# A graph layer on one core: the weight matrix multiplied to each block's sum instead of to the gathered table

## The chip, the cores and the metric

The kernel runs on 1 core of a Trainium2 chip. The metric is the device time of one execution in microseconds (us). A core has five engines that run side by side, each through its own instruction queue in order: TensorE (PE; its weight loads are listed apart as PEld), VectorE (DVE), ScalarE (ACT), GpSimd (POOL) and SyncE (SP), the last of which here only issues transfers. Engines wait for each other through semaphores.

## What is computed

Two steps on a table x of 8192 rows and 512 columns. The first is a graph layer: every row is normalised, multiplied by a 512x512 matrix, and the rows of the result are summed along 131072 weighted edges. The second is a patch: some rows (by a mask on their normalised values) send two small vectors through a 7-layer network of width 160, and a one-hot vector of its result is added to 32 columns.

```python
def _L0_gnn_ref(x, weight, row, col, vals):
    h = jnp.einsum('nf,ef->ne', x, weight)
    msgs = vals[:, None] * h[col]
    return jax.ops.segment_sum(msgs, row, num_segments=8192)

x = x + _L0_gnn_ref(_layernorm(x), L0_gnn_weight, src, dst, edge_weight)
x = x + _L0_ffn_ref(_layernorm(x)[None], L0_ffn_W, L0_ffn_b)[0]
```

All of it is in 32-bit floats. The edges come sorted by `dst` (the row that is read), and `src` (the row that is added to) is in random order, so the kernel has to sort the edges by `src` itself.

## The kernel before

**Tiling.** 128 rows make a block; there are 64 (`NB`). A block's sum over its edges is taken in 17 tiles (`FT`) of 128 edges, so 1088 tiles in all (`NT`). Eight blocks make a unit (`U`), and the network runs once for each unit.

**Stage 1, groups (L208 to L264).** The edges lie as 128 partitions x 1024. `group(q)` sorts an eighth of them into cells by block: `hot` (L211, DVE) marks for each edge its block, `p_base` (L219, PE) counts the edges of the same block on earlier partitions, `cum` (L222 to L226, ACT then DVE) ranks the edges of a partition, `p_rank` (L229, PE) picks each edge's own rank out, `slot` and `at` (L232, L234, DVE) make a one-hot of the rank. Then in four chunks of two columns each: `blocks` (L244, ACT) copies a part of `hot` to 32-bit, turned so that the 64 block marks of one edge lie next to each other; `put` (L248, DVE, twice) multiplies the one-hot by the edges' addresses (`val_a`) and by their weights (`val_w`), also turned; and 64 small matmuls (L255, PE) drop the values into their cells in `p_c`. L262 copies the cells out.

**The projection (L269 to L296).** `project(b0)` handles two blocks: loads x, statistics on DVE (L275, L276), normalises on ACT (L283), transposes on PE (L287), copies on ACT (L289), multiplies by the matrix `gw` on PE (L292), copies on ACT (L295) and stores to the table `h_rows` in HBM (L296). `some(n)` emits n such pairs: one or two behind each group, two behind each of the bits below, and the rest at the end. Up to the gather stage the order of the instructions on each engine is a scheduler's.

**Stage 2, prefix (L310 to L400).** Each row of cells is compacted: free cells are counted by a scan, each filled cell gets the distance that it has to move, and eleven rounds (L353 to L368), one for each bit of that distance, move the words and weights by powers of two: `go` (L357), `stay` (L360) and two predicated copies on DVE, and a copy on ACT (L364). Then the fields are taken apart, turned by PE transposes (L391) and copied by ACT (L393, L398) to `at_dst`, `at_row` and `at_w`: for each tile, 128 addresses, 128 target rows and 128 weights. A flag `fits` says whether every row had room; a branch on it, ahead of the gather stage, chooses between `evenly()` and a general but slow path, `anyhow()`.

**Stage 3, gathers (L611 to L664).** `evenly()` goes over the 1088 tiles in an order that is written out by hand for PE, DVE and ACT. For tile t + AHEAD it issues the gather (`fetch`, L614: an indirect DMA on POOL's queue that brings 128 rows of `h_rows`) and makes `hot` (L618, DVE: a one-hot of the target rows times the weights); for tile t it multiplies (L655, PE; a 32-bit matmul runs as two instructions). After a block's last tile DVE adds the sum to x (L658) and takes the statistics (L608). Gathered tiles and hots live in a pool of 20 buffers. Behind every fourth tile one step of the network of the unit before is emitted: `ffn` is a generator, and each `yield` ends a step.

**The network (L417 to L575).** `ffn` normalises the unit's rows, finds the masked ones and gives them slots (L503: a matmul that counts them; L525: DVE takes the slot from it; L529: a one-hot `pick`; L536: matmuls that collect the rows), `layers` runs six layers over 128 columns x 4 quarters (32 of the 160 features go through `p_b` and `hb`, 128 through `p_a` and `ha`; each layer is two steps), and the result is scattered back (`p_o`, eight matmuls), added and stored, 2 MB for each unit.

Of the kernel before, what the change touches and what calls it, by code (L numbers as in the profile page):

```python
# [9 lines left out]
F32 = mybir.dt.float32  # L10
# [24 lines left out]
def tile_gnn_ffn(  # L35
# [49 lines left out]
    h_rows = dram.tile([N, D], F32, name="h_rows")  # L85
# [24 lines left out]
    fits = const.tile([1, 1], I32, name="fits")  # L110
# [8 lines left out]
    missed = const.tile([1, 1], I32, name="missed")  # L119
# [7 lines left out]
    w_in = const.tile([P, 1, GE], F32, name="w_in")  # L127
    wo_a = const.tile([P, 1, GB], F32, name="wo_a")
# [14 lines left out]
    nc.scalar.dma_start(b_out, ffn_bT[RESULT : RESULT + 1, L - 1 : L].to_broadcast([P, 1]))  # L143
    nc.scalar.copy(wo_a[:, 0, 0:1], w_a[:, L - 1, RESULT : RESULT + 1])
# [15 lines left out]
    ps_h = cell_ctx.enter_context(tc.tile_pool(name="ps_h", bufs=1, space=PSUM))  # L160
    gw = es.tile([P, KD, D], F32, name="gw")
    nc.scalar.dma_start(gw, gnn_wT.rearrange("(k p) e -> p k e", p=P))
# [45 lines left out]
    def group(q):  # L208
# [5 lines left out]

# [7 lines left out]
        nc.scalar.copy(cum[:, :, 0, :], p_base.rearrange("p i (b g) -> p (i b) g", g=GQ))  # L222
        for c in range(1, GC):
            nc.vector.tensor_tensor(cum[:, :, c, :], cum[:, :, c - 1, :], hot[:, :, c - 1, :],
                                    OP.add)
        nc.vector.tensor_tensor(cum, cum, hot, OP.mult)  # L226
        p_rank = ps_c.tile([P, CG], F32, name="p_rank")
        for b in range(NB):
            nc.tensor.matmul(p_rank, eye, cum[:, b].rearrange("p c g -> p (c g)"),  # L229
                             start=(b == 0), stop=(b == NB - 1))  # L230
        slot = ck.tile([P, 1, CG], BF16, name="slot", bufs=2)
# [8 lines left out]
        for c0 in range(0, GC, SUB):  # L240
            cg = slice(c0 * GQ, (c0 + SUB) * GQ)
            n = SUB * GQ
            blocks = ck.tile([P, n, NB], F32, name="blocks", bufs=2)
            nc.scalar.copy(blocks, hot[:, :, c0 : c0 + SUB, :].rearrange("p b c g -> p (c g) b"))  # L244
            put = ck.tile([P, n, 2, CAP], F32, name="put", bufs=2)
            for i, val in enumerate((val_a, val_w)):
                v = val[:, q, c0 : c0 + SUB, :].rearrange("p c (g o) -> p (c g) o", o=1)
                nc.vector.tensor_tensor(put[:, :, i, :], at[:, :, cg].rearrange("p s n -> p n s"),  # L248
                                        v.to_broadcast([P, n, CAP]), OP.mult)
            for k in range(n):  # L250
# [3 lines left out]
                for h in range(2):  # L254
                    nc.tensor.matmul(  # L255
                        p_c[h * NB : (h + 1) * NB, i, gl * CAP : (gl + 1) * CAP],
                        blocks[:, k, :],
                        put[:, k, :, :].rearrange("p i (s h) -> p h i s", h=2)[:, h],
                        start=False, stop=last)
        got = p_c[:, :, :width].rearrange("p i (g w s) -> p i g w s", w=2, s=HALF)  # L260
# [8 lines left out]
    def project(b0):  # L269
        xh = hp.tile([P, HG, D], F32, name="xh")  # L270
        nc.sync.dma_start(xh, rows_of(x, b0, HG))
        mv = hp.tile([P, HG, 2], F32, name="mv_h")
        for j in range(HG):
            st = hp.tile([P, 6], F32, name="mv_h_st")
            nc.vector.bn_stats(st, xh[:, j, :])  # L275
            nc.vector.bn_aggr(mv[:, j, :], st)  # L276
        rstd = rstd_of(hp, mv[:, :, 1], HG, "rstd_h")
        nmr = hp.tile([P, HG], F32, name="nmr_h")
        nc.vector.scalar_tensor_tensor(nmr, mv[:, :, 0], -1.0, rstd, op0=OP.mult, op1=OP.mult)
        for j in range(HG):  # L280
            b = b0 + j
            xn = hp.tile([P, D], F32, name="xn")
            nc.scalar.activation(xn, xh[:, j, :], AF.Identity, bias=nmr[:, j : j + 1],  # L283
                                 scale=rstd[:, j : j + 1])
            p_t = ps_h.tile([P, KD, P], F32, name="p_t")
            for k in range(KD):
                nc.tensor.transpose(p_t[:, k, :], xn[:, k * P : (k + 1) * P], ident)  # L287
            xnT = hp.tile([P, KD, P], F32, name="xnT")
            nc.scalar.copy(xnT, p_t)  # L289
            p_h = ps_h.tile([P, D], F32, name="p_h", bufs=2)  # L290
            for k in range(KD):
                nc.tensor.matmul(p_h, xnT[:, k, :], gw[:, k, :], start=(k == 0),  # L292
                                 stop=(k == KD - 1))
            hs = hp.tile([P, D], F32, name="hs")
            nc.scalar.copy(hs, p_h)  # L295
            nc.sync.dma_start(h_rows[b * P : (b + 1) * P, :], hs)  # L296


    pairs = iter(range(0, NB, HG))

    def some(n):
        for b0 in itertools.islice(pairs, n):
            project(b0)

    for q in range(NQ):
        group(q)
        some(1 + q % 2)
# [3 lines left out]
    with tc.tile_pool(name="sq", bufs=1) as sq, tc.tile_pool(  # L311
        name="ps_q", bufs=2, space=PSUM
    ) as ps_q:
# [24 lines left out]
        nc.vector.tensor_copy(fits, good[:, 3:4])  # L338
# [13 lines left out]
        bit = LOWS + DSTS  # L352
        while bit < 32:  # L353
            s = 1 << (bit - LOWS - DSTS)

            go = sq.tile([P, ROW], I32, name="go")
            nc.vector.tensor_scalar(go, word, 31 - bit, 31, op0=OP.logical_shift_left,  # L357
                                    op1=OP.arith_shift_right)
            stay = sq.tile([P, ROW], I32, name="word", bufs=2)
            nc.vector.scalar_tensor_tensor(stay, go, -1, word, op0=OP.bitwise_xor,  # L360
                                           op1=OP.bitwise_and)
            nc.vector.copy_predicated(stay[:, : ROW - s], go[:, s:], word[:, s:])
            w2 = post.tile([P, ROW], F32, name="w2", bufs=2)
            nc.scalar.copy(w2, wt)  # L364
            nc.vector.copy_predicated(w2[:, : ROW - s], go[:, s:], wt[:, s:])
            word, wt = stay, w2
            bit += 1
            some(2)  # L368
# [33 lines left out]
    late = ctx.enter_context(tc.tile_pool(name="late", bufs=1))  # L402

# [13 lines left out]
    def layers(fp, ps_a, ps_s, v, T):  # L417

        ha = hb = None
        for i in range(L - 1):  # L420
            p_b = ps_s.tile([P, T], F32, name="p_b")
            p_a = ps_a.tile([P, NG, 512], F32, name="p_a")[:, :, :T]
# [10 lines left out]
            if i == 0:  # L433
# [5 lines left out]
                for g in range(NG):  # L439
                    r = slice(GB * g, GB * g + 3)  # L440
                    nc.tensor.matmul(p_a[:, g, :], w_in[r, 0, 0:P], v[r, :], start=True, stop=True)
# [6 lines left out]
            for g in range(NG):  # L448
                nc.tensor.matmul(p_a[:, g, :], w_b[quads[g], i, 0:P], last_hb[quads[g], :],  # L449
                                 start=True, stop=False)  # L450
            yield
            for g in range(NG):
                nc.tensor.matmul(p_b[quads[g], :], w_a[:, i, P:GE], last_ha[:, g, :],  # L453
                                 start=False, stop=True)
            evict_b()
            for g in range(NG):
                nc.tensor.matmul(p_a[:, g, :], w_a[:, i, 0:P], last_ha[:, g, :], start=False,  # L457
                                 stop=True)
# [22 lines left out]
    def ffn(fp, ps_a, ps_s, u, xu, mv):  # L481
# [70 lines left out]
        for j in range(U):  # L552
# [6 lines left out]
        addv = add.rearrange("p (h s) i -> p h (s i)", s=NPOS)  # L559
        yield  # L560
        p_o = ps_a.tile([P, U // 2, 512], F32, name="p_a")[:, :, : 32 * NPOS].rearrange(
            "p q (h c) -> p q h c", h=2)
        for j in range(U):
            q, h = divmod(j, 2)
# [56 lines left out]
    def evenly():  # L621
        AHEAD, EVERY = 4, 4
        NU = NB // U
        with tc.tile_pool(name="xp", bufs=3) as xp, tc.tile_pool(name="gp", bufs=20) as gp, \
# [20 lines left out]
            for u in range(NU):  # L645
# [14 lines left out]
                for _ in work:  # L660
                    pass
# [183 lines left out]
```

## Time and profile before

| what | us |
|---|---|
| median of 3 runs (2211.91 to 2217.22) | 2213.83 |
| the profiled execution | 2220.42 |
| its span, first to last instruction | 2218.6 |
| last group's cells copied | 373.8 |
| eleven bits | 395.1 to 518.6 |
| last store to `h_rows` issued | 598.1 |
| first gather issued | 601.4 |
| last gather issued | 2158.6 |

| engine | busy us | instructions |
|---|---|---|
| PE | 1667.6 | 9559 |
| DVE | 938.6 | 2007 |
| ACT | 376.0 | 435 |
| POOL | 1048.8 | 1110 |

In a row of groups (line, engine, operation, tile it writes, tiles it reads, shape, count) the first number behind the bar is the busy time in us and the second the mean duration of one instruction in ns; PE's instructions overlap, so busy time divided by the count is what one costs there. Behind the second bar stands the engine's idle time ahead of these instructions, and what ended most of it. "Issue" is time in which the engine waited for nothing that the profile shows; "remote" is a release by something that the trace can't name. "Granted clock" is the share of its full clock that TensorE was granted; over the whole run it was 0.89. A row of a timeline has the start in us, the duration, the instruction, and in brackets the idle time before it and its releaser.

### The profile page before, as it was taken

To read this page: it belongs to the slowest core of one execution; us is meant where nothing else is said; L and a number is where in the kernel's file an instruction comes from. 1 tells how busy PE (TensorE), PEld (TensorE's weight loads), DVE (VectorE), ACT (ScalarE), POOL (GpSimd) and SP (SyncE) were. 2 spreads that over 40 slices of the span, in tenths; PEclk is the share of its full clock that TensorE was granted. 3 is DMA by queue.
4 is the path that set the end of the run, shared out by engine and by line. 5 is a ranking of instruction groups with operands and counts; after the bars stand their busy time and mean duration, and the time that the engine had idled before them with its cause. 6 is when DMAs were issued, how large, how long until landed. Compare 5 with 4: busy or idle time off the path is not lost.

```text
span 2218.6 us, 25506 instructions
## 1 busy us (share of the span) xinstructions
PE 1667.6 (75%) x9559; PEld 823.8 (37%) x9559; DVE 938.6 (42%) x2007; ACT 376.0 (17%) x435; POOL 1048.8 (47%) x1110
## 2 busy tenths in 40 slices
PE   4888888778675858785877788587778848787784
PEld 2666665334322323332433333242333314333332
DVE  7988987995112332323233233222322322232232
ACT  3564554454200000100000010001001000100101
POOL 2000000000166666666666666666666666666660
PEclk9999999899987978897988889798889879988986
DMA  3111101222386666676686667668666766766671
GB/s 116 40 35 40 44 26 40 87 95 98 117 280 186 189 181 181 209 230 185 182 262 176 185 197 245 183 177 263 180 184 192 249 180 180 224 190 178 181 223 41
DMA packets 125196, 357.94 MB, mean 161 GB/s; under 512 B 19964, under 2 KB 21768, under 8 KB 125064
## 3 DMA queue, kind: packets, MB, share of 16 engines
q0 software_dynamic: 87040, 285.28, 43.9%
q1 hardware_dynamic: 35120, 68.69, 8.9%
q10 hardware_dynamic: 2904, 2.21, 0.3%
q8 instruction: 83, 1.36, 0.3%
q14 instruction: 49, 0.40, 0.1%
HBM read 322.55 MB, written 33.55 MB: 161 GB/s over the span
## 4 chain that ended last, share of the span: by engine, by line
PE 30%; another core or an unknown queue 24%; DVE 9%; issue 5%; DMA 2%; POOL 1%; ACT 1%; DVEq 0%; POOLq 0%; ACTq 0%
PE p_g L655 26%; DVE hot L618 4%; PE p_a L457 2%; DMA xu<-in_x_dram 1%; POOL g L614 1%; DVE xu L658 1%; DVE st L608 1%; PE p_a L449 1%; DMA g<-h_rows,at_dst 1%; PE p_b L453 1%; PE p_b L446 1%; DVE ln L492 0%; DMA out_dram<-xu 0%; PE p_v L536 0%
## 5 line engine op out<-in xcount | busy, mean ns | idle before, releaser
L614 POOL DMA_INDIRECT g<-h_rows,at_dst x1088 | 1032.7, 949 | 731.1 <-issue 240.6
L655 PE MATMUL p_g<-g,hot 128*128 128x512 f32 x2176 | 1069.9, 645 | 235.2 <-issue 98.1
L655 PEld LDWEIGHTS p_g<-g,hot 128*128 128x128 f32 x2176 | 432.9, 207 | 794.5 <-issue 603.3
L618 DVE TENSOR_SCALAR hot<-lanes,at_row,at_w 128x128 f32<-128x128 f32 x1088 | 295.0, 360 | 43.7 <-issue 43.0
L292 PE MATMUL p_h<-gw,xnT 128*128 128x512 f32 x512 | 248.4, 626 | 47.1 <-ACT xnT L289 46.9
L658 DVE TENSOR_TENSOR xu<-xu,p_g 128x512 f32<-128x512 f32 x64 | 43.9, 686 | 542.5 <-remote 317.9
L321 POOL MEMSET zero<- 128x2560 bf16 x1 | 2.2, 2231 | 360.0 <-PE p_c L255 360.0
L255 PE MATMUL p_c<-put,blocks 128*64 128x40 f32 x4096 | 131.0, 234 | 38.8 <-DVE put L248 38.8
L292 PEld LDWEIGHTS p_h<-gw,xnT 128*128 128x128 f32 x512 | 94.9, 197 | 156.5 <-issue 92.3
L428 DVE TENSOR_SCALAR hb<-p_b,b_b 128x128 f32<-128x128 f32 x48 | 16.8, 351 | 314.7 <-remote 129.1
L255 PEld LDWEIGHTS p_c<-put,blocks 128*64 128x64 f32 x4096 | 127.6, 143 | 46.0 <-issue 23.8
L149 ACT ACTIVATE rstd_f<-mv_f,eps 128x8 f32<-128x8 f32 x8 | 2.4, 300 | 815.8 <-DVE st L608 392.1
L244 ACT CAST blocks<-hot 128x2048 f32<-128x2048 bf16 x32 | 126.2, 3945 | 69.7 <-PE p_c L255 64.3
L431 ACT ACTIVATE ha<-p_a,b_a 128x512 f32<-128x512 f32 x48 | 33.0, 687 | 419.1 <-PE p_g L655 191.5
L248 DVE TENSOR_TENSOR put<-at,val_a 128x1280 f32<-128x1280 bf16 x32 | 81.0, 2531 | 0.1
L248 DVE TENSOR_TENSOR put<-at,val_w 128x1280 f32<-128x1280 bf16 x32 | 75.7, 2364 | 0.0
L295 ACT COPY hs<-p_h 128x512 f32<-128x512 f32 x64 | 37.5, 586 | 144.3 <-PE p_h L292 79.4
L275 DVE BATCH_NORM_STATS2 mv_h_st<-xh 128x6 f32<-128x512 f32 x64 | 41.9, 682 | 46.5 <-DMA xh<-in_x_dram 46.4
L446 PE MATMUL p_b<-hb,w_b 32*32 32x128 f32 x320 | 18.9, 311 | 49.8 <-DVE hb L428 49.7
L283 ACT ACTIVATE xn<-xh,nmr_h,rstd_h 128x512 f32<-128x512 f32 x64 | 52.4, 824 | 4.1 <-issue 2.3
L457 PE MATMUL p_a<-ha,w_a 128*128 128x128 f32 x320 | 49.4, 296 | 3.4 <-issue 3.4
L546 ACT COPY back<-p_v 128x256 f32<-128x256 f32 x8 | 3.0, 372 | 287.0 <-PE p_v L544 212.1
(154 smaller groups left out, 950.9 us busy)
## 6 DMA issues: line engine op xcount, KB each, us to landing
g<-h_rows,at_dst POOLq DMA_INDIRECT x1088
xh<-in_x_dram SPq DMA_DIRECT2D x32, 512.0 KB
h_rows<-hs SPq DMA_DIRECT2D x64, 256.0 KB
xu<-in_x_dram SPq DMA_DIRECT2D x16, 1024.0 KB
out_dram<-xu SPq DMA_DIRECT2D x8, 2048.0 KB
gw<-in_gnn_wT_dram ACTq DMA_DIRECT2D x1, 1024.0 KB
w_a<-in_ffn_wT_dram ACTq DMA_DIRECT2D x1, 560.0 KB
w_b<-in_ffn_wT_dram ACTq DMA_DIRECT2D x4, 140.0 KB
```

Of the source, the lines that this page charges most:

```text
L244: nc.scalar.copy(blocks, hot[:, :, c0 : c0 + SUB, :].rearrange("p b c g -> p (c g) b"))
L248: nc.vector.tensor_tensor(put[:, :, i, :], at[:, :, cg].rearrange("p s n -> p n s"), v.to_broadcast([P, n, CAP]), OP.mult)
L255: nc.tensor.matmul(p_c[h * NB : (h + 1) * NB, i, gl * CAP : (gl + 1) * CAP], blocks[:, k, :], put[:, k, :, :].rearrange("p i (s h) -> p h ...
L275: nc.vector.bn_stats(st, xh[:, j, :])
L283: nc.scalar.activation(xn, xh[:, j, :], AF.Identity, bias=nmr[:, j : j + 1], scale=rstd[:, j : j + 1])
L292: nc.tensor.matmul(p_h, xnT[:, k, :], gw[:, k, :], start=(k == 0), stop=(k == KD - 1))
L446: nc.tensor.matmul(p_b[quads[g], :], w_b[quads[g], i, P:GE], last_hb[quads[g], :], start=True, stop=False)
L457: nc.tensor.matmul(p_a[:, g, :], w_a[:, i, 0:P], last_ha[:, g, :], start=False, stop=True)
L614: nc.gpsimd.indirect_dma_start(out=g, out_offset=None, in_=h_rows, in_offset=bass.IndirectOffsetOnAxis(ap=dst_ap, axis=0))
L618: nc.vector.tensor_scalar(hot, lanes, row_ap, w_ap, op0=OP.is_equal, op1=OP.mult)
L655: nc.tensor.matmul(p_g, hot, g, start=(k == 0), stop=(k == FT - 1))
L658: nc.vector.tensor_add(xu[:, j, :], xu[:, j, :], p_g)
```

## The change

**The matrix.** The table in HBM, now `n_rows`, holds the normalised rows of x without the matrix. The block's sum in the gather stage is copied out of PSUM by ACT (`z`), turned by four PE transposes, copied by ACT again (`zT`), and multiplied by `gw` into `p_y`; DVE adds `p_y` to x and takes the statistics. These are four steps of a generator, `block`, of which one is emitted behind every fourth tile, together with one step of the network. Hots and gathers are six tiles ahead instead of four, in 16 buffers instead of 20. `gw` is loaded after the prefix.

```diff
+    def weigh(fp, ps_w, xj, z, mv, j):
+        p_t = ps_w.tile([P, KD, P], F32, name="p_t")
+        for k in range(KD):
+            nc.tensor.transpose(p_t[:, k, :], z[:, k * P : (k + 1) * P], ident)
+        zT = fp.tile([P, KD, P], F32, name="zT")
+        nc.scalar.copy(zT, p_t)
+        yield
+        p_y = ps_w.tile([P, D], F32, name="p_y")
+        for k in range(KD):
+            nc.tensor.matmul(p_y, zT[:, k, :], gw[:, k, :], start=(k == 0), stop=(k == KD - 1))
+        yield
+        nc.vector.tensor_add(xj, xj, p_y)
+        st6 = fp.tile([P, 6], F32, name="st6")
+        nc.vector.bn_stats(st6, xj)
+        nc.vector.bn_aggr(mv[:, j, :], st6)
...
-        AHEAD, EVERY = 4, 4
+        AHEAD, EVERY = 6, 4
-        with tc.tile_pool(name="xp", bufs=3) as xp, tc.tile_pool(name="gp", bufs=20) as gp, \
+        with tc.tile_pool(name="xp", bufs=3) as xp, tc.tile_pool(name="gp", bufs=16) as gp, \
-                tc.tile_pool(name="ps_g", bufs=2, space=PSUM) as ps_g, \
+                tc.tile_pool(name="ps_g", bufs=3, space=PSUM) as ps_g, \
+                tc.tile_pool(name="ps_w", bufs=1, space=PSUM) as ps_w, \
...
+            def block(u, j, xu, mv, p_g):
+                z = fp.tile([P, D], F32, name="z")
+                nc.scalar.copy(z, p_g)
+                yield
+                yield from weigh(fp, ps_w, xu[:, j, :], z, mv, j)
+                if j == U - 1:
+                    works.append(ffn(fp, ps_a, ps_s, u, xu, mv))
+            works, blocks = [], []
+            def step():
+                for gens in (blocks, works):
+                    if gens and next(gens[0], gens) is gens:
+                        gens.pop(0)
...
                         if t % EVERY == EVERY - 1:
-                            next(work, None)
-                    nc.vector.tensor_add(xu[:, j, :], xu[:, j, :], p_g)
-                    stats(fp, xu, mv, j)
-                for _ in work:
-                    pass
-                work = ffn(fp, ps_a, ps_s, u, xu, mv)
+                            step()
+                    blocks.append(block(u, j, xu, mv, p_g))
```

**The normalisation.** `project` becomes a generator `normalise` of two half steps for each pair of blocks, with the sums taken by ACT and no work for PE. One half step follows each of a group's four chunks, three follow each bit.

```diff
+    def normalise():
+        for b0 in range(0, NB, HG):
...
+            nc.sync.dma_start(xh, rows_of(x, b0, HG))
...
+            for j in range(HG):
+                nc.scalar.activation(xn[:, j, :], xh[:, j, :], AF.Identity,
+                                     accum_out=one[:, j : j + 1])
+            nc.vector.tensor_scalar(neg, one, -1.0 / D, None, op0=OP.mult)
+            for j in range(HG):
+                nc.scalar.activation(xn[:, j, :], xh[:, j, :], AF.Square, bias=neg[:, j : j + 1],
+                                     accum_out=two[:, j : j + 1])
+            yield
+            rstd = hp.tile([P, HG], F32, name="rstd_h")
+            nc.scalar.activation(rstd, two, AF.Sqrt, bias=eps, scale=1.0 / D)
+            nc.vector.reciprocal(rstd, rstd)
+            nc.vector.tensor_tensor(neg, neg, rstd, OP.mult)
+            for j in range(HG):
+                nc.scalar.activation(xn[:, j, :], xh[:, j, :], AF.Identity,
+                                     bias=neg[:, j : j + 1], scale=rstd[:, j : j + 1])
+            nc.sync.dma_start(n_rows[b0 * P : (b0 + HG) * P, :].rearrange("(b p) d -> p b d", p=P),
+                              xn)
+            yield
```

**The groups.** `group` is cut into `begin` (`hot`, `p_base`, the first column of `cum`), `rank` (the rest of `cum`, `p_rank`) and `fill` (from `slot` on), and the order is written out by hand: the next group's `begin` stands between a group's `rank` and its `fill`. `blocks` and `put` are laid out so that the copies and products read and write in order, and the matmuls that read them take every 32nd element; the product with the weights is GpSimd's.

```diff
-            blocks = ck.tile([P, n, NB], F32, name="blocks", bufs=2)
-            nc.scalar.copy(blocks, hot[:, :, c0 : c0 + SUB, :].rearrange("p b c g -> p (c g) b"))
-            put = ck.tile([P, n, 2, CAP], F32, name="put", bufs=2)
-            for i, val in enumerate((val_a, val_w)):
-                v = val[:, q, c0 : c0 + SUB, :].rearrange("p c (g o) -> p (c g) o", o=1)
-                nc.vector.tensor_tensor(put[:, :, i, :], at[:, :, cg].rearrange("p s n -> p n s"),
-                                        v.to_broadcast([P, n, CAP]), OP.mult)
+            blocks = ck.tile([P, NB, n], F32, name="blocks", bufs=2)
+            nc.scalar.copy(blocks, hot[:, :, c0 : c0 + SUB, :].rearrange("p b c g -> p b (c g)"))
+            put = ck.tile([P, 2, CAP, n], F32, name="put", bufs=2)
+            for i, (on, val) in enumerate(((nc.vector, val_a), (nc.gpsimd, val_w))):
+                v = val[:, q, c0 : c0 + SUB, :].rearrange("p (o c) g -> p o (c g)", o=1)
+                on.tensor_tensor(put[:, i], at[:, :, cg], v.to_broadcast([P, CAP, n]), OP.mult)
...
-                        blocks[:, k, :],
-                        put[:, k, :, :].rearrange("p i (s h) -> p h i s", h=2)[:, h],
+                        blocks[:, :, k],
+                        put[:, :, :, k].rearrange("p i (s h) -> p h i s", h=2)[:, h],
...
+    with tc.manual_schedule(engines={PE, DVE, ACT}):
+        begin(0)
+        for q in range(NQ):
+            p_rank = rank(q)
+            if q + 1 < NQ:
+                begin(q + 1)
+            fill(q, p_rank)
```

**The prefix.** Its order on PE, DVE and ACT is the program's too, and the operands are cut to the columns that a later bit can still read (`n` and `m` in the code). `fits` becomes `misfit`, which is read only at the end: `evenly()` always runs, and the general path follows if it is needed.

```diff
-        bit = LOWS + DSTS
-        while bit < 32:
+        bits = range(LOWS + DSTS, 32)
+        for bit in bits:
             s = 1 << (bit - LOWS - DSTS)
+            n = min(ROW, KEEP + (1 << len(bits)) - 2 * s)
+            m = min(n, ROW - s)
...
-            some(2)
+            some(3)
```

**The network.** `w_z` holds the 32 rows of `w_b` (and of `w_in`) of each quarter, zero elsewhere, so that a quarter's matmul can use all 128 rows; the part through `w_a` is one matmul of 512 columns instead of four of 128. A layer is one step instead of two. The result is scattered back by one DVE product (`apart`) and two matmuls instead of eight.

```diff
-            for g in range(NG):
-                nc.tensor.matmul(p_a[:, g, :], w_b[quads[g], i, 0:P], last_hb[quads[g], :],
-                                 start=True, stop=False)
-            yield
...
+            for c in range(0, NG * T, 512):
+                nc.tensor.matmul(fa[:, c : c + 512], w_a[:, i, 0:P], fh[:, c : c + 512],
+                                 start=True, stop=False)
             for g in range(NG):
-                nc.tensor.matmul(p_a[:, g, :], w_a[:, i, 0:P], last_ha[:, g, :], start=False,
-                                 stop=True)
+                nc.tensor.matmul(p_a[:, g, :], w_z[:, i, g, :], last_hb, start=False,
+                                 stop=((g + 1) * T % 512 == 0))
```

## The prediction

> **What bounds the kernel now.** I read the page's slices first, then the windows, the chain of waits, the groups and the timeline.
>
> ```profile
> PE 1667.6 (75%) x9559; PEld 823.8 (37%) x9559; DVE 938.6 (42%) x2007; ACT 376.0 (17%) x435; POOL 1048.8 (47%) x1110
> ...
> POOL 2000000000166666666666666666666666666660
> PEclk9999999899987978897988889798889879988986
> ...
> PE 30%; another core or an unknown queue 24%; DVE 9%; issue 5%; DMA 2%; POOL 1%; ACT 1%; DVEq 0%; POOLq 0%; ACTq 0%
> ...
> L614 POOL DMA_INDIRECT g<-h_rows,at_dst x1088 | 1032.7, 949 | 731.1 <-issue 240.6
> L655 PE MATMUL p_g<-g,hot 128*128 128x512 f32 x2176 | 1069.9, 645 | 235.2 <-issue 98.1
> ...
> L658 DVE TENSOR_TENSOR xu<-xu,p_g 128x512 f32<-128x512 f32 x64 | 43.9, 686 | 542.5 <-remote 317.9
> ```
>
> POOL's row shows two stages: none of its gathers until about a quarter of the span, then an even 6 tenths to the end. POOL's timeline gives the borders:
>
> ```profile
> 601.36 1.10 POOL L614 DMA_INDIRECT g<-h_rows,at_dst  x1 [205.65 <-SPq L841]
> 602.77 0.95 POOL L614 DMA_INDIRECT g<-h_rows,at_dst  x1 [0.30 <-issue]
> 604.02 0.94 POOL L614 DMA_INDIRECT g<-h_rows,at_dst  x1 [0.31 <-issue]
> ```
>
> The first gather is issued at 601.4 and the last at 2158.6; the span ends at 2218.6 and 1.8 us lie around it. So the profiled 2220.4 = 601.4 + 1557.2 + 60.0 + 1.8, and it stands 6.6 us (0.3%) above the median, 2213.8. One gather follows another after 1.25 us where nothing holds POOL up: 1088 x 1.25 = 1360 us is the gather stage's floor. It takes 197 us more, 3.1 us in each of 64 blocks (24.3 instead of 21.25). Windows say that PE isn't the cause:
>
> ```profile
> 500.00:600.00 100.00, 85.44 (x261) 41.11 (x259) 37.98 (x81) 41.08 (x77) 0.00 (x0) 0.98 0.26 90
> 634.00:809.00 175.00, 111.92 (x233) 45.79 (x232) 41.37 (x141) 0.00 (x0) 116.04 (x123) 0.81 0.65 187
> ...
> 1205.00:1398.00 193.00, 154.86 (x517) 66.84 (x517) 65.57 (x228) 10.73 (x17) 128.39 (x135) 0.88 0.69 206
> ```
>
> (Busy PE, weight loads, DVE, ACT, POOL; granted clock, DMA share, GB/s.) The first seven blocks run without any network steps, with 112 us of PE work in 175 us; a later unit of eight has 155 in 193. That is 25.0 and 24.1 us per block: more PE work cost no time. What holds the stage is DVE's add of a block's sum (L658), directly behind the block's last matmul, with only four hot tiles made ahead of it: 317.9 us of idle time before it, in 14 waits. The other place is a unit's hand-over from DVE to PE and back:
>
> ```profile
> 1035.13 0.16 DVE L525 TENSOR_TENSOR slot<-slot,p_v 128x8 f32<-128x8 f32 x1 [21.54 <-remote]
> ```
>
> DVE stood 21.5 us there, PE 17.5 behind it and POOL 4.0. Before 601 us the bound is a chain over DVE, ACT and PE in eight groups (to 373.8), then DVE's eleven bits (395.1 to 518.6), then, from 524.6 to 598, the rest of the projection.
>
> **The groups.** Removed: the projection's statistics, its xnT and hs evictions, 512 half matmuls and 256 half transposes, all after the change in the gather stage or gone. The new chain goes by these rows:
>
> ```profile
> L244 ACT CAST blocks<-hot 128x2048 f32<-128x2048 bf16 x32 | 126.2, 3945 | 69.7 <-PE p_c L255 64.3
> L248 DVE TENSOR_TENSOR put<-at,val_w 128x1280 f32<-128x1280 bf16 x32 | 75.7, 2364 | 0.0
> L283 ACT ACTIVATE xn<-xh,nmr_h,rstd_h 128x512 f32<-128x512 f32 x64 | 52.4, 824 | 4.1 <-issue 2.3
> L342 DVE TENSOR_TENSOR dist<-dist,free 128x2560 f32<-128x2560 f32 x1 | 2.8, 2802 | 0.0
> L364 ACT COPY w<-w 128x2560 f32<-128x2560 f32 x10 | 23.3, 2330 | 8.3 <-DVE nmr_h L279 8.3
> ```
>
> A contiguous blocks copy, by L364, is 2330 x 2048/2560 = 1.9 us (3.9 if it stays as it is); a contiguous put, by L342, 1.4 (2.4 if not). DVE's part is the cumulative sums 4.8, their product 4.4, the next hot 4.4, slot 0.3 and at 2.8: 16.7 us. ACT starts its copies about 19 us into the group and has 4 x 1.9 and two normalised pairs of 6 x 0.82 + 0.3 plus a short wait, 5.7 each: 19. The next group starts 1.7 us before that ends: 36.3, against (373 - 15)/8 = 44.8. The val_w half goes to POOL, idle there; between 1.1 us (L194's iota, 0.89 ns an element) and twice DVE's row, 4.7, it hides in a chunk (36.3/4 = 9 us); at 4.7 it would add some 3 us at a group's end, 24 in all. The first group starts at 27: the groups end at 27 + 8 x 36.3 = 318.
>
> The operands that became contiguous for ACT and DVE are strided for PE (weights by 128 bytes, moving by 256). No row has such reads. L255's matmuls take 131.0/32 = 4.1 us a chunk; unchanged, they hide; doubled, PE has 33 + 8 us of work a group and it takes about 43.8, 60 us more in all. I take the first: the nearest row is L219, whose moving operand comes in runs of 16 elements, and its 512 columns take 34.3/128 = 0.27 us, against 0.24 for L239's 320 columns in one run. Against it stands that the strided reads of DVE in L248 cost 1.8 times the contiguous 1.4; so the 60 us stay in the range.
>
> [...]
>
> **The bits.** The first head, 21 us, stays: 339. A bit has 10.5 us of DVE work (1.5 + 2.8 + 3.1 + 3.1) and now stands in hand-made order with three half steps of the normalisation, whose small DVE operations wait for ACT: after the last DVE copy at 10.5 a square pair 1.7, root and product 0.6, a scaling pair 1.7 and sums 1.7, together 16.3. Eleven are 179, less 4 for shorter operands: 514 (before, 11.2 each). If the waits hide, 55 us less; that is the low end. Then the fields, 6 us, and transposes and evictions, 27 x 0.14 + 6 x 0.58 + 6 x 0.2, with waits 10, and the last address tile's way to POOL 3: **first gather at 533** (478 to 595). The store of normalised rows is 16 MB as before, in 32 instead of 64 issues on SP, and the last lands during the fields. The branch on fits (205.7 us of POOL's idle time, but nothing ready before 598) goes: below 1 us. gw, 1 MB, is loaded behind the prefix, 35 us ahead of its first use: nothing; late, the first block would wait.
>
> **The gather stage.** POOL's 1088 issues are unchanged, so is its 1360. PE per block today: 1069.9/64 = 16.7, and 155/8 - 16.7 = 2.7 of network, both at clock 0.88: 14.7 and 2.4 at full clock. To this come L292's 248.4/64 = 3.9 at 0.98, 3.8, and L287's 40.7/64 = 0.6. The widened network layers (one matmul of 512 columns for four of 128, four of full height for four of 32 rows) add 0.3, and the skipped small ones of p_o are in it. Sum 21.8; 64 blocks are 1395 at full clock. Busier PE should be granted more than 0.88: the window 500 to 600, 85% busy, had 0.98; I take 0.95, so 22.9 x 64 = 1469.
>
> Moved: the add, from directly behind the matmuls to four tiles behind p_y, with six hots ahead; that takes the 317.9 us off the way of the hots. Added waits: transposes wait for ACT's copy of p_g, p_y for ACT's copy of p_t; behind each, on PE's queue, stand the next tiles' matmuls, and behind those POOL's buffers (16, not 20). Each has four tiles, 5.7 us, of cover for a 0.6 us copy. The eight 17 to 21 us hand-overs of a unit stay; six hots cover two tiles, 2.9 us, more. I add 6 us a unit: 48. **Stage 1517** (1360 to 1760). The tail gets two evictions, transposes, p_y and an add: 60 + 8 = 68.
>
> Sum: 533 + 1517 + 68 + 2 = 2120, by the median's scale 2114 (-4.5%).
>
> **Rivals.** (1) POOL's floor is reached: waits vanish and PE runs at full clock, 1400: 533 + 1400 + 68 + 2 = 2003. For: the rate's indifference to PE work. Against: PE and POOL would both be full, in one coupled queue. (2) Slower: PE becomes the bound through the two trips to ACT in every block. Today's trip costs 3.1 us a block though DVE, not PE, makes it. If PE stalls, its clock stays at 0.88: 21.8/0.88 = 24.8, plus 3.1 = 27.9, stage 1785, sum 2388; with half of the wait 2290. It decides from (2220 - 603)/64 = 25.3 us a block. For: 21.5 us at L525, and clock 0.81 in the first unit. Against: the cover of four tiles. (3) Strided PE operands or unchanged copies eat the groups' gain: 2120 + 60 = 2180.
>
> **How the numbers follow.** Forecast 0.42, (1) 0.13, (3) 0.13, (2) 0.28, and 0.04 that gains and losses cancel within 0.2%, about what a measurement here can tell from no change. Faster 0.68, same 0.04, slower 0.28. The likeliest case's own range is 2050 to 2190; the whole range is 2000 to 2310: half of (1) and less than half of (2) lie outside.
>
> **What would show it.** First gather near 533; groups of 36 us with blocks copies near 1.9; bits of 16; an average gather period of 1.39 us with PE over 90% busy at 0.95; no large "remote" wait at the add. Wrong if PE's p_y or p_t matmuls wait for ACT copies by microseconds in every block, if L255's successors exceed 5 us a chunk, or if the clock falls under 0.85.

## The result, and the profile after

The changed kernel takes 2334.48 us (2331.4 to 2335.17, 4 runs) beside 2214.07 us for the kernel before: a ratio of 1.054, 95% interval 1.0522 to 1.0558. It is slower by 5.4%; 2114 was forecast, with 2000 to 2310 as the range. Chips differ in the gather stage: the kernel before takes 2207 to 2239 us on some and 2019 to 2026 on others, so each run below is compared with the kernel before on its own chip.

| part of the profiled run, us | before | forecast | after |
|---|---|---|---|
| last group's cells copied (the second of its two copies; the first ends at 373.8) | 374.1 | 318 | 452.7 |
| from there to the first gather (601.4, 533, 646.2) | 227.3 | 215 | 193.5 |
| first to last gather issue | 1557.2 | 1517 | 1608.9 |
| last gather issue to the end | 60.0 | 68 | 76.8 |
| span | 2218.6 | 2118 | 2331.9 |

The page of the changed kernel (engine rows of the slices, the chain, groups):

```profile
PE   3999999600069769978996998797889789978984
...
POOL 3233222300066665666666666656666666666640
PEclk8565556555589889999998999999989999988997
...
PE 59%; another core or an unknown queue 18%; DVE 12%; issue 6%; ACT 3%; POOL 1%; DMA 1%; ACTq 0%; DVEq 0%; POOLq 0%
PE p_g L712 27%; PE p_c L268 13%; PE p_y L654 9%; PE p_a L476 2%; PE p_rank L238 2%; PE p_a L479 2%; DVE word L380 1%; DVE word L378 1%; DVE w L383 1%; DVE hot L641 1%; POOL put L262 1%; DVE at L248 1%; PE p_t L648 1%; ACT xn L296 1%
...
L712 PE MATMUL p_g<-g,hot 128*128 128x512 f32 x2176 | 996.1, 608 | 28.7 <-DVE hot L641 18.8
...
L654 PE MATMUL p_y<-gw,zT 128*128 128x512 f32 x512 | 273.0, 683 | 122.0 <-ACT zT L650 62.0
L268 PE MATMUL p_c<-put,blocks 128*64 128x40 f32 x4096 | 309.9, 350 | 32.2 <-POOL put L262 25.2
...
L262 POOL TENSOR_TENSOR put<-at,val_w 128x1280 f32<-128x1280 bf16 x32 | 117.9, 3696 | 302.5 <-DVE at L248 199.8
...
L262 DVE TENSOR_TENSOR put<-at,val_a 128x1280 f32<-128x1280 bf16 x32 | 47.7, 1490 | 72.4 <-PE p_c L268 72.1
...
L258 ACT CAST blocks<-hot 128x2048 f32<-128x2048 bf16 x32 | 62.6, 1955 | 45.8 <-PE p_c L268 45.8
```

The row of the small matmuls before the change:

```profile
L255 PE MATMUL p_c<-put,blocks 128*64 128x40 f32 x4096 | 131.0, 234 | 38.8 <-DVE put L248 38.8
```

The operands that became contiguous cost what was forecast: blocks 1.96 us (forecast 1.9), a put on DVE 1.49 (1.4), on POOL 3.7 (between 1.1 and 4.7). But the same 4096 small matmuls that took 131 us now keep PE for 310, 9.7 us a chunk instead of 4.1, and PE's clock row stands at 5 and 6 tenths where it was at 9. A group takes 51.3 us, of which 38.8 are four chunks (128 small matmuls each) back to back; most of the rest is PE's counting for this group and the next, 9.2, and a wait of 3.6 for POOL's product.

In the gather stage, from 708 us on, PE's work is done at a granted clock of 0.90 to 0.95, but PE waits for ACT's copies (122.0 us ahead of p_y). The timeline at 1037 us shows how:

```profile
1038.62 0.58 ACT L686 COPY z<-p_g 128x512 f32<-128x512 f32 x1 [23.59 <-remote]
...
1039.25 1.11 PE L648 MATMUL p_t<-ident,z 128*128 128x128 f32 x4 [7.74 <-ACT z L686]
...
1048.52 0.58 ACT L650 COPY zT<-p_t 128x512 f32<-128x512 f32 x1 [9.32 <-remote]
...
1049.16 1.22 PE L654 MATMUL p_y<-gw,zT 128*128 128x512 f32 x1 [4.38 <-ACT zT L650]
```

ACT's copy of p_g starts 11.4 us after that block's last recorded matmul ended (1027.2), and the next one 8.2 us after the four transposes. The semaphores that these copies wait for are raised by PE and by ACT itself alone, and PE's is still recorded as counting up five times from 1032.9 to 1038.5, while PE ran nothing between 1031.5 and 1039.2: its releases reach their waiters late. Over the 64 blocks the copy of p_g starts 2.6 us behind PE's last matmul for it on average, that of p_t 3.3, the add behind p_y 2.8; ACT and DVE stood idle for 2.1, 3.3 and 1.7 us of that. Before the change it was the same: DVE stood idle for over 1 us between a block's last matmul and the add behind it in 26 of 64 blocks, for up to 23.9.

### The profile page after: what moved, and what is told of

Same layout as the page of the kernel before. It is cut to its first block, busy times and chain, and to the rows that moved or that the text cites. A ratio compares the mean times of both kernels' runs of the same rounds, so it can differ in the third digit from the quotient of the medians.

```text
span 2331.9 us, 24805 instructions
## 1 busy us (share of the span) xinstructions
PE 1807.1 (77%) x9223; PEld 1018.5 (44%) x9223; DVE 857.8 (37%) x1896; ACT 411.9 (18%) x699; POOL 1171.9 (50%) x1148
## 4 chain that ended last, share of the span: by engine, by line
PE 59%; another core or an unknown queue 18%; DVE 12%; issue 6%; ACT 3%; POOL 1%; DMA 1%; ACTq 0%; DVEq 0%; POOLq 0%
PE p_g L712 27%; PE p_c L268 13%; PE p_y L654 9%; PE p_a L476 2%; PE p_rank L238 2%; PE p_a L479 2%; DVE word L380 1%; DVE word L378 1%; DVE w L383 1%; DVE hot L641 1%; POOL put L262 1%; DVE at L248 1%; PE p_t L648 1%; ACT xn L296 1%
## 5 line engine op out<-in xcount | busy, mean ns | idle before, releaser
L637 POOL DMA_INDIRECT g<-n_rows,at_dst x1088 | 1032.9, 949 | 738.9 <-issue 225.9
L712 PE MATMUL p_g<-g,hot 128*128 128x512 f32 x2176 | 996.1, 608 | 28.7 <-DVE hot L641 18.8
L712 PEld LDWEIGHTS p_g<-g,hot 128*128 128x128 f32 x2176 | 413.0, 195 | 515.1 <-issue 452.5
L654 PE MATMUL p_y<-gw,zT 128*128 128x512 f32 x512 | 273.0, 683 | 122.0 <-ACT zT L650 62.0
L268 PE MATMUL p_c<-put,blocks 128*64 128x40 f32 x4096 | 309.9, 350 | 32.2 <-POOL put L262 25.2
L268 PEld LDWEIGHTS p_c<-put,blocks 128*64 128x64 f32 x4096 | 308.7, 254 | 34.9 <-POOL put L262 34.9
L262 POOL TENSOR_TENSOR put<-at,val_w 128x1280 f32<-128x1280 bf16 x32 | 117.9, 3696 | 302.5 <-DVE at L248 199.8
L656 DVE TENSOR_TENSOR xu<-xu,p_y 128x512 f32<-128x512 f32 x64 | 43.8, 684 | 517.9 <-PE p_g L712 225.3
L654 PEld LDWEIGHTS p_y<-gw,zT 128*128 128x128 f32 x512 | 110.3, 220 | 276.9 <-issue 204.5
L258 ACT CAST blocks<-hot 128x2048 f32<-128x2048 bf16 x32 | 62.6, 1955 | 45.8 <-PE p_c L268 45.8
L304 ACT ACTIVATE xn<-xh,neg,rstd_h 128x512 f32<-128x512 f32 x64 | 49.2, 816 | 55.1 <-DVE neg L302 55.1
L296 ACT ACTIVATE xn<-xh,neg 128x512 f32<-128x512 f32 x64 | 46.2, 725 | 64.8 <-DVE neg L294 64.8
```

Of the source, the lines that this page charges most:

```text
L262: on.tensor_tensor(put[:, i], at[:, :, cg], v.to_broadcast([P, CAP, n]), OP.mult)
L268: nc.tensor.matmul(p_c[h * NB : (h + 1) * NB, i, gl * CAP : (gl + 1) * CAP], blocks[:, :, k], put[:, :, :, k].rearrange("p i (s h) -> p h ...
L296: nc.scalar.activation(xn[:, j, :], xh[:, j, :], AF.Square, bias=neg[:, j : j + 1], accum_out=two[:, j : j + 1])
L304: nc.scalar.activation(xn[:, j, :], xh[:, j, :], AF.Identity, bias=neg[:, j : j + 1], scale=rstd[:, j : j + 1])
L637: nc.gpsimd.indirect_dma_start(out=g, out_offset=None, in_=n_rows, in_offset=bass.IndirectOffsetOnAxis(ap=dst_ap, axis=0))
L654: nc.tensor.matmul(p_y, zT[:, k, :], gw[:, k, :], start=(k == 0), stop=(k == KD - 1))
```

## The experiments

**What the strided reads cost.** Two runs with the layout exchanged: e1 is the changed kernel with the old layout, e2 the kernel before with the new one. Both have both products on DVE.

```diff
-            blocks = ck.tile([P, NB, n], F32, name="blocks", bufs=2)
-            put = ck.tile([P, 2, CAP, n], F32, name="put", bufs=2)
+            blocks = ck.tile([P, n, NB], F32, name="blocks", bufs=2)
+            put = ck.tile([P, n, 2, CAP], F32, name="put", bufs=2)
...
-                        blocks[:, :, k],
+                        blocks[:, k, :],
```

> The changed kernel with blocks and put laid out as before (PE reads them in order; both products on DVE). After the change a chunk of the small matmuls into p_c takes 9.7 us, against 4.1 before, and a group 51.3 us. Theory STRIDE (the strided reads alone are slow): a chunk falls to about 4 us, PE leaves the path, DVE's 16.7 + 4 x 4.9 us and waits set a group of 41 to 45 us, first gather near 590 instead of 646. Theory CLOCK (with the projection gone PE is granted 0.55 to 0.60 of its clock in the groups, and that alone doubles the time): a chunk near 7.5 us, a group of 50 us or more, first gather 635 or later. The gather stage (1609 us from first to last gather) should stay within 15 us by both.

> The kernel before with only the new layout of blocks and put (both products on DVE), the projection still between the groups, so that PE is kept busy at a clock near 1.0. STRIDE: a chunk takes 7 us or more even at full clock, and the groups end later than 373.8 by some 20 to 60 us, total 2235 to 2275. CLOCK: a chunk stays at 4.1 us; DVE saves 1 us in each of 64 products and ACT 2 us in each of 32 copies, the groups end earlier, total 2170 to 2205.

e1: 2024.5 us beside 2021.5 for the kernel before; group 43.8 us, first gather at 585.2, so the layout is worth 61 of the 646.2 us, and the group and the first gather are as STRIDE said. A chunk fell to 6.7, not to 4: part of CLOCK holds. e2: 2161.6 beside 2021.5, first gather at 738.5: the new layout costs the kernel before 140 us, where STRIDE had 20 to 60. With PE's work in the chunks and the projection's in one queue, a group takes 59.7, and PE is busy for 58.9 of it. The small matmuls in e1 and in e2:

```profile
L269 PE MATMUL p_c<-put,blocks 128*64 128x40 f32 x4096 | 215.3, 302 | 46.9 <-ACT blocks L258 38.4
```

```profile
L254 PE MATMUL p_c<-put,blocks 128*64 128x40 f32 x4096 | 310.9, 348 | 0.5 <-DVE put L248 0.3
```

Both forecasts for e1's gather stage missed: it was 1370.5 us, not 1609. Both totals for e2 missed for the same reason: on this chip the kernel before takes 2021.5.

**What the moved work costs in the gather stage.** e3 leaves the multiplication by W out; e4 lets PE wait longer before it needs ACT's copies (each block under way then takes a step at a time):

```diff
                 nc.scalar.copy(z, p_g)
                 yield
+                yield
+                yield
                 yield from weigh(fp, ps_w, xu[:, j, :], z, mv, j)
...
         nc.scalar.copy(zT, p_t)
         yield
+        yield
+        yield
```

> The changed kernel without the multiplication by W: the block's sum is copied out by ACT and added to x, with no transposes and no p_y (the output is then not the reference's). It prices the moved work in the gather stage (1609 us now). Theory WORK (PE's own work sets the stage): PE loses 316 us of busy time and the stage falls to POOL's floor, 1360 to 1420. Theory TRIPS (PE's waits for ACT's copies, 176 us, are the loss): it falls by 176 or more, 1380 to 1430. Theory RATE (the pace of tiles is set by something else, late releases by PE, as before the change when more PE work cost nothing): it stays near the 1557 of before, 1530 to 1570.

> The changed kernel with 12 tiles instead of 4 between ACT's copies and the PE work that needs them, so that two blocks are in flight; the same instructions. TRIPS: PE's idle time ahead of p_t and p_y (54 + 122 us) goes, the stage falls from 1609 to 1440 to 1500, total 2165 to 2225. WORK: PE is idle elsewhere instead, the stage stays within 30 us of 1609. RATE: late releases go on, the waits move to DVE's hots and POOL's buffers, the stage falls by less than 60, 1550 to 1609.

Stage 1374.3 in e3 (total 2079.5) and 1369.8 in e4 (2084.9), beside 2021.5 for the kernel before. On that chip neither tells anything: the stage was at POOL's floor with the moved work and without. That e3's stage lies in WORK's range (and e4's in no range) follows from the floor and speaks for no theory. So the two kernels themselves were run again.

> The changed kernel itself, once more, beside the kernel before. In the first four experiments the kernel before took 2021.5 us instead of 2214, and the gather stage of all four lasted 1368 to 1374 us, whatever PE had to do. Theory STATE (the gather stage's surplus over 1370, 187 us before the change and 239 us after, belongs to the chip that ran it and not to the kernel): where the kernel before takes about 2021, this one takes 646 + 1370 + 70 + 2 = 2088; where it takes about 2214, this one takes about 2334. Theory WORK: the stage of this kernel stays above 1450 on every chip, since it has two more trips to ACT than the kernels with 1370; total 2170 or more.

> The kernel before, with a profile on the same chip as the other runs. STATE: first gather at about 601, as in its first profile, and the stage 1370 where the total is near 2021 or 1557 where it is near 2214; PE's releases are prompt (below 0.2 us from a block's last matmul to the add behind it) in the first case and late by up to 24 us in the second.

On one chip: changed 2078.4, before 2023.0, a ratio of 1.027 of single runs; stages 1366.5 and 1366.4. STATE holds. In the windows of the changed kernel there PE is at full clock; in the one of the kernel before, shown behind them, at 0.96:

```profile
900.00:1100.00 200.00, 197.55 (x657) 89.82 (x650) 72.44 (x241) 27.37 (x44) 151.24 (x160) 1.00 0.77 237
1100.00:1400.00 300.00, 293.58 (x931) 132.07 (x930) 107.26 (x349) 29.55 (x49) 227.37 (x239) 1.00 0.75 232
```

```profile
1205.00:1398.00 193.00, 170.73 (x547) 61.02 (x548) 63.17 (x222) 10.43 (x16) 146.10 (x155) 0.96 0.77 242
```

PE is busy 98% of the time after the change and 88% before, in these windows, and POOL's 146 to 151 us of issues in 193 to 200 us are the floor in both. Releases are prompt: the waits ahead of p_y shrink to nothing, in the page of the same run:

```profile
L654 PE MATMUL p_y<-gw,zT 128*128 128x512 f32 x512 | 230.3, 592 | 0.7 <-ACT zT L650 0.7
```

**Which operand.** The changed kernel with one operand in order at a time: e7 the weights (blocks as before), e8 the moving side (put as before, on DVE).

> The changed kernel with blocks (the weights of the small matmuls) laid out as before and put (their moving operand) in the new layout, on DVE and GpSimd. With both strided a chunk takes 9.7 us whether PE is granted 0.58 or 0.70 of its clock; with both in order 6.7 us at 0.62. Theory WEIGHTS (the strided weight loads are the slow side): a chunk near 6.5 us, a group below 44 us, first gather 530 to 580. Theory MOVING: a chunk stays at 9 us or more, first gather 630 or later.

> The reverse: put laid out as before (both products on DVE), blocks in the new layout. WEIGHTS: a chunk stays at 9 us or more, first gather 630 or later. MOVING: a chunk near 6.5 us; DVE sets a group of 41 to 44 us, first gather 565 to 590.

2022.4 and 2026.7 beside 2022.9; first gather at 586.9 and 590.3; groups of 44.5 and 44.3. The small matmuls in e7 and in e8:

```profile
L268 PE MATMUL p_c<-put,blocks 128*64 128x40 f32 x4096 | 177.9, 270 | 68.7 <-ACT blocks L258 31.9
```

```profile
L269 PE MATMUL p_c<-put,blocks 128*64 128x40 f32 x4096 | 256.5, 301 | 38.1 <-DVE neg L295 38.1
```

The clock that the trace shows over each chunk sorts the lengths (32 chunks a run, from the first start to the last end; medians of those wholly at one clock). "In order" is as before, where the moving side takes every second element. On which engine the products run makes no difference: one is on POOL in the changed kernel, none in e2, and both have 9.85.

| small matmuls | at full clock | at half clock |
|---|---|---|
| both in order (before; e1) | 3.93 us | 7.05 us |
| moving side strided (e7) | 4.80 us | 7.03 us |
| weights strided (e8) | 8.16 us | none (8.18 at 0.71 to 0.72, four chunks) |
| both strided (after; e2; also e3, e10) | 9.80 us (one chunk in e3, one in e10) | 9.85 us |

So the weights are the slow side, as WEIGHTS said, though e8's chunk lay between the two forecasts. The half clock is a loss of its own only where the weights are in order (3.93 to 7.05 us, 4.80 to 7.03): with strided weights the clock makes no difference in these runs (8.1 to 8.3 us from 0.71 to 1.0 in e8, 9.65 to 9.97 from 0.50 to 1.0 with both strided). In the changed kernel the strided operands alone are the loss; the clock counts once the weights are in order. That neither kernel gained more had another cause: in e7 DVE stood 4.3 us (L301, at 253.6) at a small operation of the normalisation, behind ACT's copies, before it could go on with the next group's counts.

**A kernel with that mended.** e9 has e7's layout; the first two blocks copies of a group go ahead of the next group's counts, a pair's normalisation is three steps, one of which follows each DVE operation of a bit, and the next pair's load is a pair ahead:

```diff
-            p_rank = rank(q)
+            early = [spread(q, 0), spread(q, SUB)]
+            p_rank = rank(q)
             if q + 1 < NQ:
                 begin(q + 1)
-            fill(q, p_rank)
+            fill(q, p_rank, early)
...
                 nc.scalar.activation(xn[:, j, :], xh[:, j, :], AF.Identity,
                                      accum_out=one[:, j : j + 1])
+            yield
             nc.vector.tensor_scalar(neg, one, -1.0 / D, None, op0=OP.mult)
```

e10 is the changed kernel with every second gather left out.

> The changed kernel with the weights of the small matmuls in order (blocks as before), and three orders mended: the first two blocks copies of a group stand on ACT ahead of the next group's counts, a normalised pair is cut into three steps so that no small DVE operation stands directly behind the ACT work that it waits for (two, two, one and two steps behind a group's chunks; one behind each of a bit's four DVE operations), and the next pair's load is issued a pair ahead. With the weights in order alone a group takes 44.5 us and a bit 14.3, and DVE waits for ACT at the small operations in both. Theory WAITS (those waits set groups and bits now that PE's chunks are short): groups of 33 to 38 us, bits near 11, first gather 470 to 510, total 1905 to 1945 beside 2022 for the kernel before. Theory ENGINE (ACT's own work is the bound: 4 x 3.9 plus three normalised pairs): groups stay at 42 us or more, total 1960 or more. By either the gather stage stays at 1367 on a chip where the kernel before takes 2022.

> The changed kernel with every second gather left out (a gathered tile is used for two tiles; the output is then not the reference's), PE's work unchanged. It shows what PE alone needs in the gather stage, now that POOL's floor of 1360 us is reached with PE 98% busy. Theory POOL (PE has slack that the floor hides): the stage falls to 1300 us or below. Theory FULL (PE's own work is as long as POOL's floor): 1330 to 1400.

Both ran on a chip where the kernel before takes 2211.7. e9: 2197.4, ratio 0.9929 (0.9902 to 0.9955), which is the same within 2%. First gather at 515.1, a bit about 11 us as WAITS said, a group 40.8, between the theories: with the chunks at half clock (7.0 us) PE is busy for 35.7 us of a group, DVE for about 29 and ACT for 27 (by the window from 100 to 300 us), which neither theory had. The gather stage was 1609.5. e10: with half the gathers the stage fell to 1276.8 us from first to last gather, as POOL said; PE's 64 blocks took 1305 us, 20.4 us each, 55 us less than POOL's floor, PE busy without a break and at full clock:

```profile
1000.00:1400.00 400.00, 400.00 (x1427) 188.68 (x1427) 143.06 (x477) 53.22 (x85) 153.64 (x162) 1.00 0.44 133
```

On this same chip its releases were prompt, 0.1 us or less for the copy of p_t in all but one block. (The total, 2533 us, has 610 us behind the last gather, most of it `again()`, which a flag starts where more rows are masked than have slots.)

**Trips or rate.** e11 is e9 with e4's extra steps, e12 has 26 buffers and 14 tiles ahead besides; e13 is e9 again. Further down e15 and e17 are e11 once more, e16 and e18 are e12.

> The combined kernel with 12 tiles instead of 4 between ACT's copies and the PE work that needs them. On a chip where the kernel before takes about 2212 (late releases), TRIPS: PE's idle time ahead of p_t and p_y goes and the stage falls from 1609 to 1430 to 1500. RATE (releases are served at a pace that the gather traffic sets, whatever waits for them): the stage stays within 40 us of 1609. On a chip where the kernel before takes about 2022 the stage is 1367 by both, total near 1950.

> The same with 26 buffers and 14 tiles ahead instead of 16 and 6. On a chip with late releases, TRIPS: what is left of POOL's and DVE's waits for buffers goes too, the stage falls below 1460. RATE: it stays within 40 us of the run with 16 buffers. On a prompt chip 1367, total near 1950.

> The combined kernel once more, on the chip of the other two. Where the kernel before takes about 2022: first gather at 515, stage 1367, tail 66, total 1948 to 1955, 3.5% faster than before. Where it takes about 2212: again 2185 to 2205.

The chip had prompt releases: stages 1367.0, 1366.2 and 1369.9; 1951.2, 1953.5 and 1948.4 us beside 2021.1. **e13 is faster than the kernel before by 3.6%** (0.9636, 0.9613 to 0.9659), with the first gather at 510.3. The extra cover gains nothing there. They were run again, together with a test of the clock: e14 puts two wide matmuls behind each chunk.

```diff
+            p_w = ps_c.tile([P, 512], F32, name="p_w")
+            for _ in range(2):
+                nc.tensor.matmul(p_w, ident, rev.rearrange("p u k -> p (u k)"), start=True,
+                                 stop=True)
```

> The combined kernel with two 32-bit matmuls of 512 columns (of constants, the result unused) behind each chunk of the small matmuls, 1.7 us of PE work at full clock, where the projection stood before the change. Theory CLOCK (the small matmuls alone don't earn the full clock; wide matmuls beside them do): the granted clock in the groups rises from 0.60 to 0.8 or more and a chunk falls from 6.85 us to 5.5 or less. Theory LENGTH (the clock follows PE's busy time, which is already 89%): the clock stays near 0.6, a chunk at 6.5 or more, a group grows from 40.8 us to 45 or more.

> As in e11: if this chip is one with late releases (the kernel before near 2212), TRIPS: stage 1430 to 1500; RATE: within 40 us of 1609. Where the kernel before takes about 2022, stage 1367, and the question stays open.

> As in e12: on a chip with late releases TRIPS gives a stage below 1460, RATE one within 40 us of the run with 16 buffers; on a prompt chip 1367.

e15 and e16 met a prompt chip again (1956.1 and 1955.5 beside 2022.6). e14: 1950.9; in the groups its window has a clock of 0.91, against 0.72 for e13:

```profile
100.00:300.00 200.00, 179.88 (x2948) 139.00 (x2948) 144.90 (x108) 134.08 (x155) 72.67 (x20) 0.91 0.19 62
```

```profile
100.00:300.00 200.00, 163.29 (x2889) 151.32 (x2884) 148.81 (x110) 135.37 (x161) 72.99 (x20) 0.72 0.19 63
```

A chunk falls from 6.3 to 5.3 us (202.6 and 168.6 us of the small matmuls in 32 chunks), as CLOCK said, and a group stays at 41.0 because the fillers take what they save: PE is busy for 36.6 us of it, 33.4 in e13. Yet e7 and e8 had 0.85 and 0.91 in the same window without these two matmuls, so what sets the clock in the groups isn't settled.

> As in e11, in case this chip has late releases (the kernel before near 2212): TRIPS: stage 1430 to 1500; RATE: within 40 us of 1609. On a prompt chip 1367, and the question stays open.

> As in e12, in case this chip has late releases: TRIPS: stage below 1460; RATE: within 40 us of the run with 16 buffers. On a prompt chip 1367.

These met late releases (the kernel before at 2238.9): 2192.9 and 2209.1, stages 1609.1 and 1610.8. RATE's range holds, though what sets the pace isn't shown: four kernels with the matrix in the gather stage have 1608.9, 1609.5, 1609.1 and 1610.8 us on such chips, with 4 or 12 tiles of cover and with 16 or 26 buffers. The lateness merely moves: in e17 each of the three copies and adds of a block starts 6.1 us behind PE's last matmul on average, where e9 had 2.4 to 3.6. PE's waits for ACT's copies, TRIPS' loss, all but go and come back ahead of p_g; here are p_y and p_g in e9, then in e17:

```profile
L670 PE MATMUL p_y<-gw,zT 128*128 128x512 f32 x512 | 278.9, 696 | 133.9 <-ACT zT L666 74.8
L728 PE MATMUL p_g<-g,hot 128*128 128x512 f32 x2176 | 988.3, 605 | 16.4 <-DMA g<-n_rows,at_dst 8.8
```

```profile
L672 PE MATMUL p_y<-gw,zT 128*128 128x512 f32 x512 | 248.0, 630 | 29.5 <-ACT zT L666 20.3
L734 PE MATMUL p_g<-g,hot 128*128 128x512 f32 x2176 | 1039.6, 622 | 116.6 <-DVE hot L657 65.7
```

A window of e17 still has PE idle for 41 of 300 us:

```profile
1100.00:1400.00 300.00, 258.95 (x747) 114.40 (x746) 88.28 (x297) 24.16 (x41) 193.60 (x204) 0.91 0.65 192
```

## Why the prediction was wrong, by its steps

**The groups: the step that failed most, 135 us.** "I take the first" was said of the strided operands, that they cost PE nothing, from L219's runs of 16 elements. That row has a strided moving side; the strided weights had no row, and they are what costs: 8.16 us a chunk at full clock (e8) against 3.93, and 9.80 with both (e3, e10). Eight groups of 51.3 instead of 36.3 us are 120 of the 135; the other 15 are the first group's alone, whose counting has no earlier group to run beside: it ended at 93.6, forecast 63.3. The bound from the other side, "doubled", fell short of the true size, 2.4 times. Rival (3) had its mechanism right and its price too low: a group of 51.3 instead of 43.8, 8 x 7.5 = 60 us short. The clock was left out too: the working carried 4.1 us a chunk over from a stage whose clock was 0.97 in the chunks, and after the change it was 0.52. With both operands strided that cost nothing (9.80 us at full clock, 9.85 at half); with the operands in order it would have cost 3 us a chunk (e1).

**The bits and the fields: right in kind.** A bit took 15.4 us of the 16.3 forecast, with DVE waiting for ACT as described; the whole stretch to the first gather took 193.5 instead of 215.

**The gather stage: 1609 instead of 1517, by the wrong model.** The working built the stage from PE's work at an assumed clock plus hand-overs. PE's work alone is 20.4 us a block (forecast 21.8), and where releases are prompt PE and POOL run side by side at the floor of 1367, near rival (1)'s 1400. Where they are late, the pace is 24.3 us a block before and 25.1 after, whatever PE has to wait for. "More PE work cost no time" was seen and then not used: by that reading the stage would have stayed at 1557. Where the 51.7 us over it come from isn't shown: e3, which leaves the matrix out, ran on a prompt chip alone. The claim that the add's 317.9 us could be taken off the way failed: with the add moved, the stage grew, and on a prompt chip the kernel before has its floor with the add where it was (1366 us), so those waits were the effect of late releases and not the cause of the pace. Rival (2) had the sign for a chip like that one; its price, a stage of 1785, missed, and its cause, the trips, is refuted by e17 and e18.

**The tail** took 76.8 instead of 68, and 65 on chips with prompt releases.

**The sum of it.** 135 - 22 + 92 + 9 = 214 us, from 2118 to 2332. On the prompt chip of e5 and e6 the change loses 2.7%, all of it ahead of the first gather and in the tail: 46 us at 645.3 against 599.2, and 9 us at the end.

Still open: what makes releases late on some chips, and with it why the gather stage took 92 us more than forecast. Shown is that in one run with half the gathers on such a chip (e10) they were prompt, and that the trace of a late run has far fewer separate records of the gathers' completions: 409 to 581 for each of eight counters before the change, against 2170 to 2179 in the prompt run of the same kernel (e6). Why either is so, no run measured.

## What to carry to other kernels

An operand that is laid out for the engine that writes it can be paid for by the one that reads it, here 8.16 us a chunk instead of 3.93: price the strided weight load of every small matmul before the copy that it saves, and look at the granted clock of the stage from which a duration is taken. Where an engine waits for a matmul that ended long before by the records (11.4 us before the copy of p_g above), more cover and more buffers only moved the wait here: the stage took 1609.5 us in e9, 1609.1 in e17 and 1610.8 in e18. Before a stage is costed, its floor should be looked for on more than one chip.

## What the runs showed that was not expected

A small DVE operation took longer beside a POOL product: the 128x2 scaling `neg` took 903 ns on average in the changed kernel, and 168 ns in e1, where both products are on DVE. In the changed kernel the 16 that ran at the same time as a POOL product took 0.89 to 2.55 us, the other 16 at most 0.17.

```profile
L294 DVE TENSOR_SCALAR neg<-one 128x2 f32<-128x2 f32 x32 | 28.9, 903 | 61.4 <-ACT xn L292 61.4
```

The same program differs by 9% between chips (2212 and 2022 us for the kernel before), and nearly all of it is in the gather stage: 1557 against 1366 us, while each gather's issue takes 0.95 us on both (949 ns in the profile of before, 952 in e6).
